# Down's first half with the seven-product scheme applied twice, weights held in the array and results turned in squares of 32

## The chip, the cores and the metric

The kernel runs on one core of one Trainium2 chip. The metric is device time in microseconds of one execution, as a median over runs. Of the core's engines, TensorE (PE in the profile) multiplies, loading one 128x128 operand into its array (PEld, "held" or "stationary" below) and streaming the other through it; VectorE (DVE), ScalarE (ACT) and GpSimd (POOL) do elementwise work; SyncE (SP) issues the DMAs here, in the order of its queue. Everything is float32.

## The reference

Eight blocks of 512 tokens by 512 features. Cut to what matters:

```python
xn = layernorm(x)
# linear attention
q, k, v = (einsum("bld,ed->ble", xn, W) + b for W, b in ((Wq, bq), (Wk, bk), (Wv, bv)))
kv = cumsum((elu(k) + 1) * v, axis=1)
s = einsum("bld,ed->ble", (elu(q) + 1) * kv * 32 ** -0.5, Wo) + bo
# gated feed-forward, 512 -> 2 x 2048 -> 512, each input rotated by signs and a Hadamard transform
h = fwht(xn * SU_ug) / 64
h = silu(h @ W_gate.T * (scale_gate * 64)) * (h @ W_up.T * (scale_up * 64))
g = fwht(h * SU_dp) / 64 @ W_down.T * (Wscale_dp * 64)
out = x + s * silu(g)
```

The kernel folds signs, transforms and the Down scales into the weights as it starts, so that each projection is one matrix product. "Down" is the product with `W_down`: 2048 hidden features in, 512 out.

## The kernel before

The eight blocks are worked in four pairs, p = 0 to 3; pairs follow each other without a break. In a pair come the attention's projections, four hidden units u = 0 to 3 (each is a gate and an up projection for a quarter of the hidden features, SiLU and product), the output projection after u = 0, the first half of Down after u = 1 (`down(p, 0, ...)`, over the hidden features of units 0 and 1), and the second half after u = 3, which adds the first half's result, applies the gate and writes the output.

All large products go by the seven-product scheme: a product of 2x2 blocks with 7 instead of 8 block products, named P1 to P7 (`P1, P2, P7, P3, P4, P5, P6 = range(7)`, L18). Each operand is kept as its seven "factors" (blocks, sums and differences of blocks), and running sums of products give the four result blocks.

The scheme is used at one or two levels:

- *Hidden units of pairs 1 to 3* (`by_blocks`, L947, and `block_product`, L678, matmul at L686) use two levels: seven outer products, each of seven inner ones. Weights are held and tokens stream. An outer product's inner sums sit in three PSUM tiles `px`, `py`, `pz`; `px` collects P1, P6, P5, P3 one on top of another and is read out in between by `read` (ScalarE copy, or VectorE addition where an earlier outer product is to be added), and `output` adds such a reading and `py` or `pz` into the result (L691 to L727). Results lie features by tokens.
- *Down* (`down`, L1001, through `token_groups`, L568, matmul at L584) uses one level: 7 products x 4 blocks of the contraction x 2 token groups x 2, each matmul 128x128 by 128x256. Here the tokens are held and the weights stream, so that results lie tokens by features, as input and output do. In the first half the sums are read by ScalarE copies (L593) and added by VectorE in 128x512 pieces (L599). The two finished results `dn`, 1 MB each, go to DRAM by one DMA each (`put_by`, L881), and are fetched for the second half (`fetch`, L886).

What a hidden unit leaves, `ho` (L983 to L991), is a tile of two feature blocks x seven token factors x 512 tokens. After each outer product `gated` (L985) is called for a finished result: SiLU on ScalarE, product and subtractions on GpSimd, or on VectorE for the last ones of a unit that stands ahead of Down. `by_blocks` itself has two sums on GpSimd, `u3 = u1 + v` (L961) and `v += r` (L965).

*Order of work.* The instructions of an engine run in program order, and a list `agenda` (L475 to L492) decides the order: `at(place, fn)` puts a step some number of places ahead, `advance(n)` runs the steps up to a place; one place is about a block product. `pace`, `later` and `nearest` slip waiting VectorE work in behind given instructions. `block_product` puts its seven products at places 0, 2, 3, 4, 8, 12 and 13 and advances by 7 only, so that products of neighbouring outer products mix and VectorE has time to empty a sum.

*Weights* come from DRAM, in the order of `queue` (L1219): `get_w` (L1259) asks for three ahead, `stream_w` (L341) issues the load on SP into the pool `wpool` of four buffers. A factor of the hidden units' weights (`w_gu`) is 896 KB, one of Down's (`w_down`) 512 KB.

*Pools.* `t8` has six 1 MB tiles, for the results and the sums; `xin` has one tile `x`, through which each block of tokens passes to be normalized (`normalized`, L190: load, layernorm on VectorE, store to `d_x`). Those tokens come back turned by 32x32 squares: `next_tokens` (L245) loads `z` in pieces of 128 bytes (32 values), and VectorE transposes each 32x32 square, which together turn the block. The loads of `z` are 256 KB each.

In pair 1, while Down's first half runs, `factors_kv` (L440) makes the second-level factors of the key and value weights: loads of `d_k` and `d_v`, seven stores to `d_kv` per part of which four wait for VectorE's sums.

## Time and profile before

| what | us |
|---|---|
| median of 3 runs (1535.12, 1537.55, 1537.87) | 1537.55 |
| the profiled execution | 1536.37 |
| its span | 1534.5 |
| granted TensorE clock, mean | 0.997 |
| Down's first half in pair 1, 2, 3: stretch of the trace | 627.96 to 678.89, 986.50 to 1037.40, 1345.00 to 1396.00 |
| median landing of a `w_gu` load (896 KB) / a `w_down` load (512 KB) | 4.5 / 4.6 |
| median landing of a `z` load (256 KB in 128-byte pieces) | 6.1 |
| median landing of a `d_d` store (1 MB) / its fetch | 7.4 / 5.7 |

The page gives each engine's busy time over the span and in 40 equal slices, the chain of work that ended last, and groups of instructions by line with their busy time, the mean duration of one, the idle time before them and what ended it. A float32 matmul appears as two records. The profiled execution is 1.2 us under the median.

### The profile page before, as it was taken

The numbers are of one execution on the slowest core, as the hardware profiler recorded it, in microseconds if no ns is written. First come the engines' busy times: TensorE is split into PE (matmuls) and PEld (weight loads), VectorE is DVE, ScalarE is ACT, GpSimd is POOL, SyncE is SP. The second block draws the span as 40 slices with busy tenths as digits, with TensorE's granted clock in tenths as the row PEclk, the third lists the DMA queues.
The fourth block names the chain that finished last, engine by engine and source line by source line (L and its number), as shares of the span: only waits on it lengthen the run. The fifth ranks groups of instructions, "written<-read, shape, count | busy, mean of one in ns | idle before, by whom it ended". The sixth has DMA issues, their size and how long they took to land.

```text
span 1534.5 us, 16212 instructions
## 1 busy us (share of the span) xinstructions
PE 1513.9 (99%) x6092; PEld 1154.2 (75%) x6092; DVE 1046.2 (68%) x1571; ACT 414.7 (27%) x668; POOL 360.5 (23%) x188
## 2 busy tenths in 40 slices
PE   7999999999999999999999999999999999999998
PEld 3446546747874688888885888888886888888887
DVE  8999788469777665636767895715675697633673
ACT  4462341232125411112115232111212332111211
POOL 1000000000320261205511235302621128200631
PEclk9999999999999999999999999999999999999999
DMA  8345778798975244784586644335484443525462
GB/s 275 96 149 170 237 273 238 228 300 280 271 282 141 96 145 176 239 275 164 167 269 217 188 144 162 116 119 182 172 247 154 142 144 113 185 93 183 160 259 81
DMA packets 213726, 288.93 MB, mean 188 GB/s; under 512 B 57488, under 2 KB 169360, under 8 KB 209424
## 3 DMA queue, kind: packets, MB, share of 16 engines
q1 hardware_dynamic: 213504, 287.87, 58.7%
q8 instruction: 48, 0.79, 0.2%
q14 instruction: 30, 0.25, 0.1%
q10 hardware_dynamic: 144, 0.03, 0.0%
HBM read 205.42 MB, written 82.44 MB: 188 GB/s over the span
## 4 chain that ended last, share of the span: by engine, by line
PE 82%; DVE 11%; DMA 4%; issue 1%; ACT 1%; POOL 0%; SPq 0%; POOLq 0%; DVEq 0%; ACTq 0%
PE px_gu L686 17%; PE px_dn L584 12%; PE pz_gu L686 9%; PE pz_dn L584 6%; PE py_gu L686 4%; PE py_dn L584 4%; PE px_kv L686 3%; PE px_o L584 3%; PE px_q L508 3%; PE px_gate L508 2%; PE pz_o L584 2%; PE pz_kv L686 2%; PE pz_q L508 2%; PE px_k L508 1%; PE px_v L508 1%
## 5 line engine op out<-in xcount | busy, mean ns | idle before, releaser
L686 PE MATMUL px_gu<-xo,w_gu 128*128 128x256 f32 x1456 | 348.4, 380 | 0.7 <-DVE sa_gu L696 0.6
L686 PEld LDWEIGHTS px_gu<-xo,w_gu 128*128 128x128 f32 x1456 | 275.2, 190 | 44.3 <-issue 2.4
L961 POOL TENSOR_TENSOR u_gu<-u_gu,v_gu 128x1024 f32<-128x1024 f32 x26 | 61.2, 2376 | 753.0 <-DVE u_gu L727 697.5
L584 PE MATMUL px_dn<-w_down,ho 128*128 128x256 f32 x1024 | 228.8, 379 | 0.9 <-DVE ho L93 0.9
L584 PEld LDWEIGHTS px_dn<-w_down,ho 128*128 128x128 f32 x1024 | 194.5, 190 | 29.4 <-issue 1.9
L686 PE MATMUL pz_gu<-xo,w_gu 128*128 128x256 f32 x728 | 187.4, 380 | 0.5 <-DVE u L524 0.4
L686 PEld LDWEIGHTS pz_gu<-xo,w_gu 128*128 128x128 f32 x728 | 137.6, 190 | 21.2 <-DVE a_gu L700 0.9
L584 PE MATMUL pz_dn<-w_down,ho 128*128 128x256 f32 x496 | 112.5, 379 | 0.6 <-DVE u L524 0.6
L584 PEld LDWEIGHTS pz_dn<-w_down,ho 128*128 128x128 f32 x496 | 93.8, 190 | 15.4 <-issue 1.2
L686 PE MATMUL py_gu<-xo,w_gu 128*128 128x256 f32 x364 | 93.7, 379 | 0.0
L1018 POOL TENSOR_TENSOR s<-s,d 128x512 f32<-128x512 f32 x30 | 40.0, 1332 | 166.0 <-ACT d L1017 166.0
L686 PEld LDWEIGHTS py_gu<-xo,w_gu 128*128 128x128 f32 x364 | 69.2, 190 | 9.4
L965 POOL TENSOR_TENSOR v_gu<-v_gu,r_gu 128x1024 f32<-128x1024 f32 x26 | 60.8, 2361 | 22.8 <-DVE r_gu L727 22.8
L508 PE MATMUL px_q<-xo,w_q 128*128 128x512 f32 x128 | 59.8, 593 | 0.3 <-ACT sa_q L520 0.3
L584 PE MATMUL px_o<-w_o,co 128*128 128x256 f32 x256 | 59.2, 380 | 0.3 <-DVE sa_o L595 0.3
L1017 ACT ACTIVATE d<-d 128x512 f32<-128x512 f32 x31 | 19.5, 630 | 144.9 <-DVE d L599 124.7
L584 PE MATMUL py_dn<-w_down,ho 128*128 128x256 f32 x256 | 57.9, 379 | 0.0
L989 ACT ACTIVATE a_gu<-a_gu,cols_sb 128x512 f32<-128x512 f32 x26 | 18.6, 720 | 142.2 <-DVE a_gu L727 140.8
L983 POOL TENSOR_TENSOR ho<-ho 128x1024 f32<-128x1024 f32 x24 | 56.3, 2357 | 1.4
L584 PEld LDWEIGHTS px_o<-w_o,co 128*128 128x128 f32 x256 | 48.3, 190 | 8.9 <-issue 1.0
L989 ACT ACTIVATE u_gu<-u_gu,cols_sb 128x512 f32<-128x512 f32 x52 | 36.6, 719 | 67.8 <-DVE u_gu L727 64.9
L584 PEld LDWEIGHTS py_dn<-w_down,ho 128*128 128x128 f32 x256 | 48.6, 190 | 6.6
(322 smaller groups left out, 2403.5 us busy)
## 6 DMA issues: line engine op xcount, KB each, us to landing
w_gu<-d_gu SPq DMA_DIRECT2D x91, 896.0 KB, 4.5
w_down<-d_down SPq DMA_DIRECT2D x56, 512.0 KB, 4.6
w_kv<-d_kv SPq DMA_DIRECT2D x14, 896.0 KB, 4.6
d_s<-o SPq DMA_DIRECT2D x8, 1024.0 KB, 6.3
d_d<-dn SPq DMA_DIRECT2D x8, 1024.0 KB, 7.4
d<-d_d SPq DMA_DIRECT2D x8, 1024.0 KB, 5.7
s<-d_s SPq DMA_DIRECT2D x8, 1024.0 KB, 8.7
y<-in_x_dram SPq DMA_DIRECT2D x8, 1024.0 KB, 7.6
```

The costliest lines, as they stand in the source:

```text
L508: nc.tensor.matmul(p.rearrange("p a t -> p (a t)") if len(r.shape) == 2 else p, ws[k][:, i, :], r, start=(first and k == 0), stop=(k == n ...
L584: nc.tensor.matmul(p[:, c], t[:, (2 * g + c) * P : (2 * g + c + 1) * P], ws[i](k), start=(first and k == 0 and c == cs[0]), stop=(k == n - ...
L686: nc.tensor.matmul(p[:, lane], w[:, lane, i, :], x[:, i, :], start=(first and lane == 0), stop=True, skip_group_check=True,)
L961: nc.gpsimd.tensor_tensor(r[:, m], ru1[:, m], rv[:, m], ALU.add)
L965: nc.gpsimd.tensor_tensor(rv[:, m], rv[:, m], rr[:, m], ALU.add)
L983: eng.tensor_tensor(ho[:, :, c], ho[:, :, a], ho[:, :, b], ALU.subtract)
L989: nc.scalar.activation(g[:, m], g[:, m], AF.Silu, scale=col("w_gate", u + m * NU + a * NG))
L1017: nc.scalar.activation(d, d, AF.Silu)
L1018: (nc.vector if final and (a, s) == (1, 0) else nc.gpsimd).tensor_tensor(r, r, d, ALU.mult)
```

## The change

For p = 1, 2, 3 Down's first half no longer calls `down(p, 0, ...)` but `down_by_blocks(p, ...)`. It applies the scheme twice, through the same `block_product`: seven outer products (in the order `IN_TURN`) of seven inner ones of two matmuls each (`two_terms`). The weights are now held and the tokens stream; a sum is 128x256 (one "lane"). Pair 0 and the second halves stay as they are.

- The second-level factors of the weights, `dl`, seven of 896 KB, are made once, in pair 1's attention (`factors_down`, at places 7, 20, 33, ...): for each, four loads of 128 KB out of `d_down`, four VectorE operations on 128x256, and one store. They pass through the tile `x` of `xin`.
- The second-level factors of the tokens are made in place in `ho`, and in halves of two `t8` tiles: per outer product n three subtractions of 128x512 and one more (`last_factor`), on GpSimd, except the first three for n = 1, which are on VectorE. Those of n = 0 stand ahead of the end of hidden unit 1.
- Sums over outer products: `read` and `output` on 128x256, and two additions of 128x1024 on VectorE (`with_u1`, `with_r`).
- Results now lie features by tokens. `turned` lets VectorE transpose each 32x32 square (two operations of 128x512 for each of four results) into a part of `ho` that is free, and eight DMAs for each result, of 64 KB in pieces of 128 bytes, put the squares at their places in `d_d`, which is now laid out tokens by features; `fetch` reads it accordingly.

```diff
@@ -16,6 +16,7 @@
 P1, P2, P7, P3, P4, P5, P6 = range(7)
+IN_TURN = (P1, P5, P6, P2, P7, P3, P4)
 @with_exitstack
@@ -345,6 +346,9 @@
             nc.sync.dma_start(w, inner[u][:, i])
         elif name[0] == "kv":
             nc.sync.dma_start(w, inner["kv"][:, name[1]])
+        elif name[0] == "dl":
+            assert name[1] in down_made
+            nc.sync.dma_start(w, inner["dl"][:, name[1]])
         elif name[0] == "down":
             h, i = name[1]
             assert wd_made[h] == 4
@@ -470,6 +474,34 @@
         at(8, plain)
         at(14, make)
+    down_made = set()
+    def factors_down(i):
+        if "dl" not in inner:
+            inner["dl"] = dram.tile([P, 7, 2, 7, P], F32, tag="d_dl", name="d_dl")
+        t = xin.tile([P, 3, 7, P], F32, tag="x", name=f"f_dl_{i}")
+        w = t.rearrange("p c s e -> p (c s e)")[:, : 2 * 7 * P].rearrange("p (m s e) -> p m s e", m=2, s=7)
+        for c in range(2):
+            for u in range(2):
+                nc.sync.dma_start(
+                    w[:, :, (P1, P2, P7, P4)[2 * c + u]], wd[0][:, i, 2 * u : 2 * u + 2, c * P : (c + 1) * P]
+                )
+        def encode():
+            for o, a, b, op in (
+                (P5, P7, P4, ALU.add), (P6, P5, P1, ALU.subtract), (P3, P2, P6, ALU.subtract), (P7, P1, P7, ALU.subtract)
+            ):
+                later(0.42, nc.vector.tensor_tensor, w[:, :, o], w[:, :, a], w[:, :, b], op)
+            later(0.0, store)
+        def store():
+            nc.sync.dma_start(inner["dl"][:, i], w)
+            down_made.add(i)
+        at(6, encode)
     agenda = []
@@ -675,21 +707,32 @@
         between()
-    def block_product(name, w, x, out, add, done, time=0):
-
-
-        px, py, pz = (bank(t, name, 2) for t in ("px", "py", "pz"))
-        sums = {}
-
+    def two_lanes(w, x):
         def product(p, i, first):
             for lane in range(2):
                 nc.tensor.matmul(
                     p[:, lane], w[:, lane, i, :], x[:, i, :],
                     start=(first and lane == 0), stop=True, skip_group_check=True,
                 )
+        return product
+    def two_terms(w, x):
+        def product(p, i, first):
+            for k in range(2):
+                nc.tensor.matmul(
+                    p[:, 0], w[:, k, i, :], x(k, i),
+                    start=(first and k == 0), stop=(k == 1), skip_group_check=True,
+                )
+        return product
+    def block_product(name, product, lanes, out, add, done, time=0):
+        px, py, pz = (bank(t, name, 2)[:, :lanes] for t in ("px", "py", "pz"))
+        sums = {}
         def read(what, m, q):
-            s = snap.tile([P, 2, H], F32, tag="s", name=f"{what}_{name}")
+            s = snap.tile([P, 2, H], F32, tag="s", name=f"{what}_{name}")[:, :lanes]
             if add is None:
                 nc.scalar.copy(s, px)
             else:
@@ -885,7 +928,8 @@
     def fetch(name):
         t = t8.tile([P, NT, D], F32, tag="t", name=name)
-        nc.sync.dma_start(t.rearrange("p n d -> p (n d)"), kept[name])
+        d = kept[name]
+        nc.sync.dma_start(t, d.rearrange("(n p) d -> p n d" if d.shape[0] == L else "p (n d) -> p n d", n=NT))
         return t
@@ -950,7 +994,7 @@
             return t8.tile([P, 2, 2, 2, H], F32, tag="t", name=f"{what}_{p}_{name}")
         def outer(i, out, add=None, done=None):
-            block_product(f"{name}_{p}_{i}", weights(i), xo[:, i], out, add, done, time)
+            block_product(f"{name}_{p}_{i}", two_lanes(weights(i), xo[:, i]), 2, out, add, done, time)
         ra = new("a")
         rest = {}
@@ -1045,6 +1089,107 @@
         if half == 0:
             for s in range(2):
                 put_by(f"d_{p}_{s}", ds[s])
+    def down_by_blocks(p, hos, get_w):
+        ds = [dram.tile([L, D], F32, tag=f"d_d_{p}_{s}", name=f"d_d_{p}_{s}") for s in range(2)]
+        h0, h1 = hos
+        room = []
+        def halves(what):
+            t = t8.tile([P, 2, 4 * H], F32, tag="t", name=f"{what}_{p}_dl")
+            return [t[:, i] for i in range(2)]
+        def result(t):
+            return t.rearrange("p (m l q t) -> p m l q t", m=2, l=1, q=2)
+        def block(a, q, o):
+            return (h0, h1)[a][:, :, o, q * H : (q + 1) * H]
+        places = {}
+        def factors(n):
+            o = IN_TURN[n]
+            eng = nc.vector if n == 1 else nc.gpsimd
+            if n < 3:
+                r = room[n].rearrange("p (i m t) -> p i m t", i=2, m=2)
+                x, y = r[:, 0], r[:, 1]
+            else:
+                x, y = (block(0, q, IN_TURN[n - 3]) for q in range(2))
+            b = block
+            eng.tensor_tensor(x, b(1, 1, o), b(0, 1, o), ALU.subtract)
+            eng.tensor_tensor(b(0, 1, o), b(0, 1, o), b(0, 0, o), ALU.subtract)
+            eng.tensor_tensor(y, b(1, 1, o), b(0, 1, o), ALU.subtract)
+            places[n] = {
+                P1: b(0, 0, o), P2: b(1, 0, o), P7: x, P6: y, P5: b(0, 1, o), P3: b(1, 1, o), P4: b(1, 0, o)
+            }
+        def last_factor(n):
+            b = block(1, 0, IN_TURN[n])
+            nc.gpsimd.tensor_tensor(b, b, places[n][P6], ALU.subtract)
+        stored = []
+        def turned(t, a, s):
+            o = (P5, P1)[len(stored) // 2]
+            z = h1[:, len(stored) % 2, o : o + 2]
+            stored.append((a, s))
+            def store():
+                d = ds[s].rearrange("(i t) (c j f) -> j t c i f", t=32, j=4, f=32)
+                for m in range(2):
+                    for j in range(4):
+                        nc.sync.dma_start(
+                            d[j][:, 2 * a + m],
+                            z[32 * j : 32 * j + 32, m].rearrange("p (i f) -> p i f", f=32),
+                        )
+            for m in range(2):
+                at(1 + 2 * m, lambda m=m: nc.vector.transpose(z[:, m], t[:, m, 0].rearrange("p q t -> p (q t)")))
+            at(4, store)
+        def outer(n, out, add=None, done=None):
+            i = IN_TURN[n]
+            w = get_w("dl", i)
+            block_product(
+                f"dl_{p}_{i}", two_terms(w, lambda k, j: places[n][j][:, k]), 1, out, add, done, 1.5
+            )
+        u3, f0 = halves("u3")
+        room.append(f0)
+        factors(0)
+        at(0, lambda: room.extend(halves("xy")))
+        at(0, lambda: factors(1))
+        at(3, lambda: factors(2))
+        for n in range(3, 7):
+            at(7 * n - 7, lambda n=n: factors(n))
+        for n in range(7):
+            at(7 * n + 5, lambda n=n: last_factor(n))
+        ra, rv = halves("a")
+        ru1, rr = halves("u1")
+        ra, rv, ru1, rr, u3 = (result(t) for t in (ra, rv, ru1, rr, u3))
+        def plus(o, a, b):
+            o, a, b = (t.rearrange("p m l q t -> p (m l q t)") for t in (o, a, b))
+            nc.vector.tensor_tensor(o, a, b, ALU.add)
+        def with_u1():
+            plus(u3, ru1, rv)
+        def with_r():
+            plus(rv, rv, rr)
+            turned(rv, 1, 1)
+        outer(0, ra)
+        outer(1, rv)
+        outer(2, ru1, ra, with_u1)
+        outer(3, ra, ra, lambda: turned(ra, 0, 0))
+        outer(4, rr, ru1, with_r)
+        outer(5, u3, u3, lambda: turned(u3, 0, 1))
+        outer(6, ru1, rr, lambda: turned(ru1, 1, 0))
+        between()
+        for s in range(2):
+            kept[f"d_{p}_{s}"] = ds[s]
     def load_y(p, s):
         y = t8.tile([P, NT, D], F32, tag="t", name=f"y_{p}_{s}")
@@ -1232,7 +1377,10 @@
                 at_o = len(queue) - (2 if p == 0 else 0)
                 queue[at_o:at_o] = [(p, "o", 0), (p, "o", 1)]
             if u % 2:
-                queue += [(p, "down", (u // 2, i)) for i in (P1, P7, P2, P6, P5, P3, P4)]
+                if p and u == 1:
+                    queue += [(p, "dl", i) for i in IN_TURN]
+                else:
+                    queue += [(p, "down", (u // 2, i)) for i in (P1, P7, P2, P6, P5, P3, P4)]
     ahead = []
     def ask(n):
@@ -1347,6 +1495,9 @@
         if p:
             catch_up()
             inner_tokens(xo)
+            if p == 1:
+                for n, i in enumerate(IN_TURN):
+                    at(7 + 13 * n, lambda i=i: factors_down(i))
             co = hop.tile([P, 2, 7, L], F32, tag="h", name=f"co_{p}")
         heads_made = (attention if p < 2 else attention_by_blocks)(p, xo, co, get_w)
         more = p + 1 < B // 2
@@ -1387,7 +1538,10 @@
                     for i, (m, lo, hi) in enumerate((("k", 0, 4), ("k", 4, 7), ("v", 0, 4), ("v", 4, 7))):
                         at(2 + 12 * i, lambda m=m, lo=lo, hi=hi: factors_kv(m, lo, hi))
                 flush()
-                down(p, 0, hos, get_w)
+                if p:
+                    down_by_blocks(p, hos, get_w)
+                else:
+                    down(p, 0, hos, get_w)
                 hos = []
         flush()
         ds = [fetch(f"d_{p}_{s}") for s in range(2)]
```

## Prediction

> **What bounds the kernel now.** I read the page's first two parts, then the chain, the groups, and windows over the three stages that change.
>
> ```profile
> span 1534.5 us, 16212 instructions
> PE 1513.9 (99%) x6092; PEld 1154.2 (75%) x6092; DVE 1046.2 (68%) x1571; ACT 414.7 (27%) x668; POOL 360.5 (23%) x188
> PE   7999999999999999999999999999999999999998
> PE 82%; DVE 11%; DMA 4%; issue 1%; ACT 1%; POOL 0%; SPq 0%; POOLq 0%; DVEq 0%; ACTq 0%
> ...
> L584 PE MATMUL px_dn<-w_down,ho 128*128 128x256 f32 x1024 | 228.8, 379 | 0.9 <-DVE ho L93 0.9
> ```
>
> TensorE (PE) is busy throughout: nothing but matmul work can be saved, and what is saved stays saved only while the other engines keep up. The clock row reads 9 in every slice. The windows of Down's first half in pairs 1, 2 and 3 (columns: us; busy us and instructions of PE, PEld, DVE, ACT, POOL; clock; DMA share; GB/s) say the same:
>
> ```profile
> 627.96:678.89 50.93, 50.93 (x237) 44.78 (x236) 21.88 (x31) 7.46 (x12) 2.00 (x1) 1.00 0.76 236
> 986.50:1037.40 50.90, 50.90 (x238) 44.74 (x237) 13.88 (x17) 7.46 (x12) 2.07 (x1) 1.00 0.39 124
> 1345.00:1396.00 51.00, 51.00 (x238) 44.83 (x237) 13.86 (x17) 7.00 (x12) 1.49 (x1) 1.00 0.39 126
> ```
>
> The reader is to see that in the second and third, VectorE (DVE) is a quarter busy and GpSimd (POOL) idle; in pair 1 the encoding of the kv weights runs beside, with DVE at 43% and DMA at 0.76.
>
> **Removed: 14 matmuls a pair.** Before: 7 products x 4 contraction blocks x 2 token groups x 2 = 112 matmuls of 128x256. After: 7 outer x 7 inner x 2 terms = 98, same shape. A row's mean includes overlap, so I take the pitch, from the chain of waits inside the stage (start us, length):
>
> ```profile
> 654.88 17.27 PE px_dn L584 x80
> ```
>
> 80 records in 17.27 us are 0.2159 a record; an fp32 matmul leaves two records (the group L584 shows 1024 for 512 matmuls), so 0.4318 us. 14 x 0.4318 = 6.05 us a pair, 18.1 us in all. Weight loads become as many as the matmuls, as before. Nothing else in PE's work changes.
>
> **Start of each stage.** The first products need hidden unit 1 finished and folded a second time. The new factor operations stand on POOL between the adds L961 and L965 of unit 1, before "v += r", which delays the last SiLU, product and subtractions; outer 1's factors then follow on DVE. From the DVE rows before (L991 at 629.63 for 1.40 us, then L983) and POOL's 1.22 us, I placed these by hand in pair 1: PE finds an output not drained (0.3), a Y sum late (0.15) and two second-outer factors late (0.7). About 1.2 us a pair, 3.6 in all; zero to 2.5 a pair for the range.
>
> **POOL: 25 subtractions of 128x512 a pair, 3 more on DVE.** The nearest rows:
>
> ```profile
> 497.34 1.27 POOL L316 TENSOR_TENSOR co<-co 128x512 f32<-128x512 f32 x1 [2.96 <-DVE co L791]
> 498.57 1.26 POOL L318 TENSOR_TENSOR co<-co 128x512 f32<-128x512 f32 x1
> 499.79 1.27 POOL L317 TENSOR_TENSOR co<-co 128x512 f32<-128x512 f32 x1
> ...
> L1018 POOL TENSOR_TENSOR s<-s,d 128x512 f32<-128x512 f32 x30 | 40.0, 1332 | 166.0 <-ACT d L1017 166.0
> ```
>
> Back to back the pitch is 1.225; the L1018 mean, beside a busier DVE, is 1.33; single ones reach 1.64 and 2.19. 25 x 1.225 = 30.6 us lie in a stage of some 44 us. The tight place is the fifteenth: at 1.225 the third outer's last factor is ready some 1.5 us before PE wants it (about 650.5 against 652 in pair 1's times). At 1.33 it is 1.6 us later, even. I take nothing; at 1.6 us an operation the lateness is 15 x 0.375 - 1.5 = 4.1 us a pair. PE is what waits then, and the rest of the stage with it.
>
> **DVE.** Five outers read their sums with 7 additions of 128x256, two with 3 (the other reads are ScalarE copies, at 0.37 by L285): 41 x 0.42 = 17.2 us. Two additions of 128x1024 at 1.215 make 2.4, eight transposes at 0.683 make 5.5, the three factors 2.0 (0.68 each, the 128x512 addition): 27 us, where six additions of 0.69 stood (4.1).
>
> ```profile
> L307 DVE TENSOR_TENSOR xo<-xo 128x256 f32<-128x256 f32 x28 | 11.3, 419 | 9.0 <-PE pz_q L508 7.2 <-PE px_q L508 1.4 <-PE py_q L508 0.4
> L93 DVE STREAM_TRANSPOSE xo<-z 128x512 f32<-128x512 f32 x24 | 15.4, 683 | 0.0
> L983 DVE TENSOR_TENSOR ho<-ho 128x1024 f32<-128x1024 f32 x28 | 33.5, 1215 | 0.3
> ```
>
> In pairs 2 and 3, 13.9 + 23 = 37 us of some 45: hidden, since an inner product's two matmuls take 0.86 us and the list spaces an outer's products so that a drain has a product or more of time. In pair 1, 21.9 + 23 = 45 of 45: no room. Overlapped issue (pitch 0.60 where the 128x512 row says 0.69) gives back some 5 us.
>
> **Making the weights, once in pair 1's attention.** Per factor four loads of 128 KB, four DVE additions of 0.42 and a store of 896 KB; 28 x 0.42 = 11.8 us of DVE, beside PE in slices where DVE shows 6 or 7 tenths. They occupy the single `x` tile, which moves the loads and layernorms of blocks 4 and 5 (about 5.2 us of DVE each) into hidden unit 0 and the output projection, and the `z` loads of block 4 (128-byte pieces, 256 KB each) into the changed stage. The matmuls cover it; uncovered it would be 22 us. I put 1 us (0 to 4).
>
> **Weights and stores.** A pair's seven Down weights grow from 512 to 896 KB. Results leave by 32 stores of 64 KB in 128-byte pieces, four batches of eight, and on SP's queue after the batches stand, one each, the loads of unit 2's weights P5, P6, P2 and P7: SP takes its queue in order, so a batch whose transpose is late, or whose predecessors are still landing, holds up that load and then PE. No store before has pieces this small. Nearest rows:
>
> ```profile
> w_gu<-d_gu SPq DMA_DIRECT2D x91, 896.0 KB, 4.5
> ...
> z<-d_x SPq DMA_DIRECT2D x24, 256.0 KB, 6.1
> ...
> d_kv<-f_k SPq DMA_DIRECT2D x7, 256.0 KB, 4.2
> ```
>
> Four `z` loads in 128-byte pieces at 763 to 772 moved 145 to 147 GB/s with full DMA; so a 512 KB batch takes 512/145 = 3.6 us, within an outer's 98/7 x 0.4318 = 6.05. By hand the four weight loads land 2 to 4 us early. The other end: pieces at twice the price, 7.2 us a batch, over the period; the loads then come later by 4 us or so a pair, 8 in pair 1.
> The Trainium skill's page "DMA: Bandwidth & Descriptors", section Specifications, speaks against the change: it gives 512 bytes as the smallest transfer at line rate, with a read-modify-write below. The `z` row shows the lower rate for loads; no row here shows a store. If the rule means two passes for a store, the sum would be that of the stores' rival below.
>
> In pair 1 DMA is the fuller term. 236 GB/s x 50.93 us = 12.0 MB; seven times 384 KB of weights (2.75 MB) makes 14.8, of which 2.1 MB go at 145 GB/s (14.5 us) and the rest at 360 GB/s, which that stretch reaches in its best slices (35 us): 50 us against 45. DVE waits there for `d_kv` stores to land (7.9 us idle in 640 to 648, harmless so far), and behind those waits now stand the drains PE needs. Some stores may slip past the stage, so 0 to 5 us; I take 2.5.
>
> **Sum.** -18.1 + 3.6 + 1 + 2.5 = -11.0. The profiled execution's 1536.37 becomes 1525.4; the median shown, 1537.55, lies 1.2 above it, so 1526.5.
>
> **Rivals.**
> - *All of it comes through.* For: PE at 100% in the windows, POOL idle there, DVE a quarter busy. Against: the late factors at the start. 1537.55 - 18.1 = 1519.5.
> - *POOL sets the pace.* With DVE at 80% or more beside it, an operation takes 1.6 us; 3 x 4.1 = 12.4 us of waits: 1539. For: the single rows of 1.64 and 2.19, beside DVE work. Against: the mean of 1.33, which alone gives 0.4 us or so more. At 1.45 us it is 1526.5 + 3 x 1.9 = 1532.
> - *The 128-byte stores hold up unit 2's weights* (the slower side). Place: PE's first product of gu_2 on each of P5 to P7. Price: pieces at twice the loads' cost, 4.4 + 4.4 + 8 = 17 us: 1543.5. It decides from where a batch takes over 6 us, and turns the sign where it costs over 11 us. For: no such store is in the trace, `z` runs at a third of the weight loads' rate. Against: the weights are asked 4 us ahead.
> - *It does not do what it says:* the matmuls replaced are counted above, so only a second use of the new weights in the wrong place could leave the saving out; excluded by the code.
>
> **Chances.** 0.2% (3.1 us) is about what a measurement of this kernel tells from no change. The forecast's case 0.44 (its own range 1522.5 to 1532); all saved 0.14; POOL 0.17, of which a bit over half ends within 3 us of before and the rest faster; stores, with DMA in pair 1 worse than 5 us, 0.25, nearly all slower. Faster: 0.44 + 0.14 + 0.07 = 0.65; same 0.11; slower 0.24. The range: below, half of the all-saved case; above, up to 1542, which leaves out some 0.12 of the stores' case.
>
> **What would show it.** Matmuls fewer by 42 (84 records); the three stages some 44 to 47 us instead of 51; PE's waits for DVE of about 1 us at each stage's start and none on POOL; drains of 128x256 at 0.42; POOL at 1.23 to 1.33; the store batches under 6 us from issue to landing; in pair 1 waits of up to 5 us, in 2 and 3 below 2. PE waiting for a `w_gu` DMA just behind the stage means the stores' rival; for POOL in the third and fourth outer, POOL's; waits in pair 1's attention or hidden unit 0 would put the making of the weights above its 1 us.

## The result and the profile after

The changed kernel takes 1560.11 us (median of 4 runs, 1559.11 to 1563.46) against 1536.89 for the kernel before (4 runs): a ratio of 1.0156, 95% interval 1.0138 to 1.0175. It is slower by 23 us where 11 us less was forecast, and above the top of the forecast's range, 1542. The page of the changed kernel:

```profile
span 1557.8 us, 16546 instructions
PE 1507.0 (97%) x6008; PEld 1139.2 (73%) x6008; DVE 1143.8 (73%) x1743; ACT 408.0 (26%) x668; POOL 472.0 (30%) x263
...
PE 71%; DVE 14%; DMA 4%; POOL 3%; SPq 3%; issue 2%; ACT 2%; POOLq 0%; DVEq 0%; ACTq 0%
```

PE has 84 records fewer, the 42 matmuls that the change removes. They are worth 18.1 us, yet the span is 23.3 longer: 41 us were lost. In the chain, POOL and SP's queue now stand with 3% each where they had nothing. What PE waited for (us in total, times, longest):

```profile
PE px_gu L713 <- DMA w_gu<-d_gu: 6.8, 3, 2.7
PE pz_o L616 <- DVE u_gu L743: 5.3, 1, 5.3
PE px_gu L713 <- DVE sc_gu L739: 3.7, 4, 1.1
PE pz_dl L722 <- DVE a_dl L743: 3.0, 3, 1.0
PE py_dl L722 <- DVE a_dl L743: 2.0, 2, 1.0
PE pz_gu L713 <- DVE u_gu L743: 1.8, 3, 0.6
PE px_dl L722 <- ACT sc_dl L737: 1.4, 3, 0.5
PE px_dl L722 <- DVE xy_dl L1122: 1.1, 3, 0.4
PE pz_dl L722 <- POOL ho L1129: 1.1, 1, 1.1
```

Three groups are to be seen: a single wait of 5.3 at the output projection (`pz_o`), three waits for weights of a hidden unit, and small waits for VectorE that come three times, once a pair. The timeline puts a place to each. I compare three stretches of both traces: pair 1 from its first key product to its first Down matmul; and, for each of pairs 1 to 3, from the first matmul of Down's first half to the first of its second half, which takes in hidden units 2 and 3 ("the long stretch" below).

| stretch, us | before | after | difference |
|---|---|---|---|
| pair 1, keys to Down | 448.77 to 627.96: 179.19 | 447.65 to 634.72: 187.07 | +7.9 |
| long stretch, pair 1 | 627.96 to 760.99: 133.03 | 634.72 to 783.06: 148.34 | +15.3 |
| long stretch, pair 2 | 986.57 to 1119.60: 133.03 | 1008.16 to 1142.06: 133.90 | +0.9 |
| long stretch, pair 3 | 1344.48 to 1477.51: 133.03 | 1366.91 to 1500.81: 133.90 | +0.9 |

With 6.05 us of matmuls gone from each long stretch, pairs 2 and 3 lost 6.9 each and pair 1 lost 21.4 there, besides the 7.9 in its attention and hidden units 0 and 1. (The rest of the two spans differs by -1.7 us in all, -1.1 of it before pair 1.) So three losses need an explanation: one that every pair has, one that only pair 1's Down has, and the making of the weights.

**The loss of every pair** lies at the stage's start. Windows over pair 3 (us; busy us and instructions of PE, PEld, DVE, ACT, POOL; clock; DMA share; GB/s):

```profile
1344.48:1366.91 22.43, 22.43 (x105) 19.75 (x104) 17.54 (x27) 2.16 (x3) 14.80 (x8) 1.00 0.48 160
1366.91:1390.30 23.39, 18.41 (x77) 13.78 (x76) 20.29 (x22) 5.77 (x12) 18.13 (x11) 1.00 0.36 118
1390.30:1416.20 25.90, 25.90 (x121) 22.80 (x120) 16.82 (x36) 0.37 (x1) 17.26 (x14) 1.00 0.64 172
```

All of it is in the middle row: PE idle for 5.0 of 23.4 us, and 77 records where 23.39 / 0.2159 = 108 fit, 6.7 us of work. VectorE and GpSimd are both busy there. What they do, first VectorE, then GpSimd, from the timeline (start, duration, line):

```profile
1369.62 2.25 DVE L1035 TENSOR_TENSOR ho<-u_gu 128x1024 f32<-128x1024 f32 x1 [1.81 <-ACT u_gu L1033]
...
1372.40 1.21 DVE L1027 TENSOR_TENSOR ho<-ho 128x1024 f32<-128x1024 f32 x1
1373.53 0.67 DVE L743 TENSOR_TENSOR u_gu<-sc_gu,pz_gu 128x512 f32<-128x512 f32 x1
1374.13 3.10 DVE L1027 TENSOR_TENSOR ho<-ho 128x1024 f32<-128x1024 f32 x2
1377.16 1.75 DVE L1120 TENSOR_TENSOR xy_dl<-ho,ho 128x512 f32<-128x512 f32 x1
1378.83 0.41 DVE L743 TENSOR_TENSOR a_dl<-sa_dl,py_dl 128x256 f32<-128x256 f32 x1
1379.16 1.42 DVE L1121 TENSOR_TENSOR ho<-ho 128x512 f32<-128x512 f32 x1
```

```profile
1368.43 2.36 POOL L1035 TENSOR_TENSOR ho<-v_gu 128x1024 f32<-128x1024 f32 x1 [0.83 <-ACT v_gu L1033]
1373.75 1.27 POOL L1129 TENSOR_TENSOR ho<-ho,u_dl 128x512 f32<-128x512 f32 x1 [2.96 <-PE px_gu L713]
1376.18 2.18 POOL L1120 TENSOR_TENSOR xy_dl<-ho,ho 128x512 f32<-128x512 f32 x1 [1.16 <-DVE ho L1027]
1378.43 1.59 POOL L1121 TENSOR_TENSOR ho<-ho 128x512 f32<-128x512 f32 x1
```

Lay the two on one another. VectorE's L1035 begins at 1369.62, while GpSimd's L1035 runs until 1370.79; from there to its end at 1371.87 is 1.08, about its duration alone (1.21). GpSimd's L1120 begins at 1376.18 while VectorE's second L1027 runs until 1377.23, and ends 1.13 later; VectorE's L1120 begins at 1377.16, and ends 0.55 after GpSimd's has ended at 1378.36. Each waits for the other's running instruction. The L743 rows in between take 0.67 and 0.41 as always: they read one operand from PSUM. So these instructions, which take both operands from SBUF, *take turns* on the two engines, one whole instruction at a time. In the kernel before, GpSimd had 2 us of work in these stages, and the two met once, for 0.35 us (its L991 is the changed kernel's L1035, its L983 the L1027):

```profile
1344.12 2.38 POOL L991 TENSOR_TENSOR ho<-v_gu 128x1024 f32<-128x1024 f32 x1 [0.83 <-ACT v_gu L989]
...
1346.15 1.42 DVE L991 TENSOR_TENSOR ho<-u_gu 128x1024 f32<-128x1024 f32 x1 [0.79 <-ACT u_gu L989]
...
1349.83 2.35 DVE L983 TENSOR_TENSOR ho<-ho 128x1024 f32<-128x1024 f32 x2
```

The rest of the changed kernel's trace says the same. Of VectorE's tensor_tensor instructions with both operands in SBUF, those that began with more than 0.25 us of a GpSimd operation still to run took 1.41 to 2.26 us for 128x1024 (19 of them) and 1.10 to 1.75 for 128x512 (14); all others took at most 1.23 and 0.69. With one operand in PSUM, 298 of 128x512 and 59 of 128x256 began so, and none took more than 0.69 and 0.43.

**The making of the weights.** The `x` tile is taken, and the layernorm of block 4 comes while the output projection runs, beside three 128x1024 subtractions of GpSimd. VectorE, then GpSimd:

```profile
565.11 0.75 DVE L155 TENSOR_SCALAR x<-x,mv,rstd 128x512 f32<-128x512 f32 x1
565.78 0.68 DVE L627 TENSOR_TENSOR sa_o<-px_o,bo_r 128x512 f32<-128x512 f32 x1
566.38 6.93 DVE L155 TENSOR_SCALAR x<-x,mv,rstd 128x512 f32<-128x512 f32 x3
573.23 0.68 DVE L770 TENSOR_TENSOR u_gu<-px_gu,r_gu 128x512 f32<-128x512 f32 x1
```

```profile
565.65 7.38 POOL L1027 TENSOR_TENSOR ho<-ho 128x1024 f32<-128x1024 f32 x3
```

L155 has a median of 0.54; here three take 6.93, one for each of GpSimd's instructions (7.38 / 3 = 2.46). The drains behind them (L770, then L743) come 5 us late, and PE stands at `pz_o` for 5.3. The clock then is not full (windows of the same trace):

```profile
560.00:580.00 20.00, 14.68 (x58) 12.27 (x57) 14.91 (x17) 7.45 (x9) 16.60 (x8) 0.83 0.43 145
690.00:710.00 20.00, 14.91 (x58) 12.07 (x57) 8.72 (x16) 3.41 (x6) 0.00 (x0) 0.88 0.99 231
```

At 0.2159 us a record 92.6 fit into 20 us. The 58 of the first window are 34.6 too few, 7.5 us of work, for 5.3 us of idle time: the granted clock, 0.83 on average, takes the rest.

**The loss of pair 1's Down.** The second of these windows shows it: PE waits for `w_gu`. SP's queue there (start, time of the issues):

```profile
679.10 0.81 SPq L346 DMA_DIRECT2D w_gu<-d_gu  x1
679.96 1.47 SPq L452 DMA_DIRECT2D f_v<-d_v  x2
681.52 8.15 SPq L1142 DMA_DIRECT2D d_d<-ho  x8
689.78 1.02 SPq L458 DMA_DIRECT2D d_kv<-f_v  x2
690.89 0.50 SPq L346 DMA_DIRECT2D w_gu<-d_gu  x1
691.48 1.30 SPq L458 DMA_DIRECT2D d_kv<-f_v  x2
692.83 7.20 SPq L1142 DMA_DIRECT2D d_d<-ho  x8
700.07 1.62 SPq L458 DMA_DIRECT2D d_kv<-f_v  x3
701.79 0.47 SPq L346 DMA_DIRECT2D w_gu<-d_gu  x1
```

The loads of `w_gu` leave 11.8 and 10.9 us apart, where an outer product, of a hidden unit as of Down, has 7 x 2 matmuls and lasts 6.05: the weights come at about half the pace at which PE can use them. A batch of eight stores holds the queue for 7 to 8 us and kv stores for 1 to 3 more. Whether it is the pieces, the bytes or the number of DMAs is for the runs.

### The profile page after: what moved, and what is told of

Its sections match the earlier page's. It is cut to its first block, busy times and chain, and to the rows that moved or that the text cites. A ratio compares the mean times of both kernels' runs of the same rounds, so it can differ in the third digit from the quotient of the medians.

```text
span 1557.8 us, 16546 instructions
## 1 busy us (share of the span) xinstructions
PE 1507.0 (97%) x6008; PEld 1139.2 (73%) x6008; DVE 1143.8 (73%) x1743; ACT 408.0 (26%) x668; POOL 472.0 (30%) x263
## 4 chain that ended last, share of the span: by engine, by line
PE 71%; DVE 14%; DMA 4%; POOL 3%; SPq 3%; issue 2%; ACT 2%; POOLq 0%; DVEq 0%; ACTq 0%
PE px_gu L713 13%; PE px_dn L616 7%; PE pz_gu L713 6%; PE py_gu L713 3%; PE pz_dn L616 3%; PE px_q L540 3%; PE px_kv L713 3%; PE px_o L616 3%; PE px_gate L540 2%; PE px_dl L722 2%; PE py_dn L616 2%; PE px_up L540 2%; PE pz_o L616 2%; PE pz_kv L713 2%; PE px_k L540 1%
## 5 line engine op out<-in xcount | busy, mean ns | idle before, releaser
L1005 POOL TENSOR_TENSOR u_gu<-u_gu,v_gu 128x1024 f32<-128x1024 f32 x26 | 61.2, 2373 | 630.7 <-DVE u_gu L770 569.7
L713 PEld LDWEIGHTS pz_gu<-xo,w_gu 128*128 128x128 f32 x728 | 139.2, 192 | 23.3 <-DVE u_gu L743 3.8
L616 PE MATMUL px_dn<-w_down,ho 128*128 128x256 f32 x640 | 143.0, 379 | 1.8 <-DVE ho L94 1.8
L616 PEld LDWEIGHTS px_dn<-w_down,ho 128*128 128x128 f32 x640 | 121.5, 190 | 20.3 <-DVE ho L94 2.2
L722 PE MATMUL px_dl<-ho,w_dl 128*128 128x256 f32 x300 | 75.1, 386 | 3.0 <-ACT sc_dl L737 1.4
L616 PE MATMUL pz_dn<-w_down,ho 128*128 128x256 f32 x304 | 69.1, 379 | 0.6 <-DVE u L556 0.6
L722 PEld LDWEIGHTS px_dl<-ho,w_dl 128*128 128x128 f32 x300 | 57.2, 193 | 14.0 <-ACT sc_dl L737 2.6
L1009 POOL TENSOR_TENSOR v_gu<-v_gu,r_gu 128x1024 f32<-128x1024 f32 x26 | 60.9, 2363 | 18.2 <-DVE r_gu L770 18.2
L616 PEld LDWEIGHTS pz_dn<-w_down,ho 128*128 128x128 f32 x304 | 57.5, 190 | 10.3 <-issue 1.2
L1027 POOL TENSOR_TENSOR ho<-ho 128x1024 f32<-128x1024 f32 x24 | 56.6, 2367 | 1.4
L737 ACT COPY sa_gu<-px_gu 128x512 f32<-128x512 f32 x26 | 15.1, 581 | 157.9 <-PE px_gu L713 129.1
```

The lines of the kernel that those rows point to most:

```text
L616: nc.tensor.matmul(p[:, c], t[:, (2 * g + c) * P : (2 * g + c + 1) * P], ws[i](k), start=(first and k == 0 and c == cs[0]), stop=(k == n - ...
L713: nc.tensor.matmul(p[:, lane], w[:, lane, i, :], x[:, i, :], start=(first and lane == 0), stop=True, skip_group_check=True,)
L722: nc.tensor.matmul(p[:, 0], w[:, k, i, :], x(k, i), start=(first and k == 0), stop=(k == 1), skip_group_check=True,)
L737: nc.scalar.copy(s, px)
L1005: nc.gpsimd.tensor_tensor(r[:, m], ru1[:, m], rv[:, m], ALU.add)
L1009: nc.gpsimd.tensor_tensor(rv[:, m], rv[:, m], rr[:, m], ALU.add)
```

## The experiments

Each line gives the median, the ratio to the kernel before on the same chip with its interval, and the long stretches of pairs 1, 2, 3 (before: 133.0 each; changed kernel: 148.3, 133.9, 133.9). "Keys to Down" is pair 1's first stretch (before 179.2, changed kernel 187.1).

**e1, only the making.**

```diff
-                if p and u == 1:
+                if False and u == 1:
...
-                if p:
+                if False:
                     down_by_blocks(p, hos, get_w)
```

> The weights' second-level factors are made in pair 1 as in the changed kernel, but every pair keeps the one-level Down. Theory 1 (layernorm of block 4, moved beside GpSimd's products in the output projection, costs its 5.3 us wait and the slow clock after it): about 1545 us, 8 over before, with the same wait of PE at pz_o. Rival (the making is hidden, all of the loss is in the new stage): 1537 to 1539. My recorded forecast for this part was 1 us.

1545.87, 1.0056 (1.0036 to 1.0076); stretches 133.1, 133.0, 133.0; keys to Down 186.9. The making alone costs 7.7 us there, with the wait of 5.3 at `pz_o` and three L155 in 6.93 as before. The rival falls.

**e2, the making in another tile.**

```diff
-        t = xin.tile([P, 3, 7, P], F32, tag="x", name=f"f_dl_{i}")
...
+        t = t8.tile([P, NT, D], F32, tag="t", name=f"f_dl_{i}")
...
```

> The changed kernel with the weights' factors made in a tile of the result pool instead of the single tile x, so that blocks 4 and 5 are normalized where they were before. Theory 1: the 5.3 us wait at pz_o goes, and the loads of z leave pair 1's new stage; 1552 if only the first matters, 1545 if the z loads also were what delayed the w_gu weights. Rival (the place of the layernorm does not matter): 1560.

1555.78, 1.0126 (1.0105 to 1.0146); keys to Down 181.5, so 5.5 of the 7.9 are gone with the wait at `pz_o`. Pair 1's long stretch is 147.0: the displaced loads of `z` had no more than 1.3 us of it.

**e3, the stores in pieces of 2 KB.**

```diff
-                d = ds[s].rearrange("(i t) (c j f) -> j t c i f", t=32, j=4, f=32)
+                d = ds[s].rearrange("(n p) d -> p n d", p=P)
...
-                            d[j][:, 2 * a + m],
-                            z[32 * j : 32 * j + 32, m].rearrange("p (i f) -> p i f", f=32),
+                            d[32 * j : 32 * j + 32, 2 * a + m], z[32 * j : 32 * j + 32, m]
```

> The 32 stores of each pair write the same bytes from the same tiles in pieces of 2 KB, so the squares are not put in place and the result differs. Theory 2 (the 128-byte stores delay unit 2's weights in pair 1): the three waits for w_gu (6.8 us) and the low clock after them go, 11 us less, 1549; pairs 2 and 3 do not change. Rival (DMA in pair 1 is full of kv factors, z and larger weights whatever the pieces): 1556 to 1560.

1558.91, 1.0141 (1.0122 to 1.0159); 146.5, 133.9, 133.9. The size of the pieces is worth 1.9 us in pair 1 and nothing in the others. My forecast's rival had the place right and the cause wrong. The rule of the Trainium skill that I weighed against the change (page "DMA: Bandwidth & Descriptors", section Specifications: no line rate below 512 bytes) hardly shows in the time here.

**e4, the new stage in pairs 2 and 3 only** (`if p > 1` in the two places of e1).

> Pair 1 keeps the one-level Down; pairs 2 and 3 use the new one; the weights are made in pair 1 as in the changed kernel. Theory: before + 8 (the making) + 2 x 0.9 (each later pair loses 6.9 us to waits against 6.05 saved): 1547. Rival (each new stage costs a third of the 23 us, 7.7 us): 1552.

1546.55, 1.0066 (1.0042 to 1.0091); 133.2, 133.9, 133.9; keys to Down 185.7. The losses add up from separate places.

**e5, the kv factors later.**

```diff
-                        at(2 + 12 * i, lambda m=m, lo=lo, hi=hi: factors_kv(m, lo, hi))
+                        at(52 + 12 * i, lambda m=m, lo=lo, hi=hi: factors_kv(m, lo, hi))
```

> The changed kernel with the kv weights' factors of pair 1 begun 50 places later, behind the new stage, in hidden units 2 and 3. Theory 2b (what pair 1's new stage loses beyond the others is that DMA and VectorE are full there with kv factors, not the 128-byte pieces): pair 1's stage with the two units behind it falls from 148.3 to about 134 us, as in pairs 2 and 3, the waits for w_gu go, and the whole is 1546. Rival (the larger weights and stores alone are too much for DMA right behind attention): stays over 1555.

1565.81, 1.0193 (1.0178 to 1.0209); 154.5, 133.9, 133.9. The waits for `w_gu` are gone, and pair 1 runs from its first Down matmul to unit 2's first in 49.3 us, as pairs 2 and 3 do (52.6 in the changed kernel). So the kv factors beside the new stage are what sets pair 1 apart. But in units 2 and 3 they cost more than they did: PE waits some 14 us there for drains that come late on VectorE. Most stand behind L465, which waits for its stores to land, and of which the last two take 4.13 beside GpSimd's L1027 (0.57 each alone); the longest wait, 5.3, lies behind a sum of GpSimd's (L1005) that is late itself. Moved, not solved.

**e6 and e7, GpSimd's subtractions left out.**

```diff
+            if n in (1,):
                 eng.tensor_tensor(x, b(1, 1, o), b(0, 1, o), ALU.subtract)
                 eng.tensor_tensor(b(0, 1, o), b(0, 1, o), b(0, 0, o), ALU.subtract)
                 eng.tensor_tensor(y, b(1, 1, o), b(0, 1, o), ALU.subtract)
+            else:
+                x, y = b(1, 1, o), b(0, 1, o)
```

(The indentation of the three lines is not shown as a change. e7 has `(0, 1)`; the last factors go with theirs, in e6 all seven.)

> GpSimd's 25 second-level token subtractions of each pair are left out (raw blocks are used in their place); VectorE's three remain. Theory 3 (GpSimd and VectorE slow each other when both read and write SBUF, and the first GpSimd operations also delay the end of unit 1): in pairs 2 and 3 VectorE's L1027 is back at 1.21 and L1120 to L1122 at 0.7, the seven waits at the stage's start go, stage with the units behind it from 133.9 to 127.5 us; whole some 1545 or less. Rival (PE waits because the two-matmul products are too short for VectorE's drains): 132 or more.

1539.79, 1.0025 (1.0016 to 1.0035); 141.5, 128.05, 128.05. VectorE in pair 3 of e6:

```profile
1354.44 1.42 DVE L1035 TENSOR_TENSOR ho<-u_gu 128x1024 f32<-128x1024 f32 x1 [0.79 <-ACT u_gu L1033]
...
1358.11 2.35 DVE L1027 TENSOR_TENSOR ho<-ho 128x1024 f32<-128x1024 f32 x2
1360.39 0.68 DVE L1121 TENSOR_TENSOR xy_dl<-ho,ho 128x512 f32<-128x512 f32 x1
1360.99 0.41 DVE L743 TENSOR_TENSOR a_dl<-sa_dl,py_dl 128x256 f32<-128x256 f32 x1
```

The same instructions: 2.25 is 1.42, 3.10 is 2.35, 1.75 is 0.68. The stage is 5.0 us shorter than before the change, of 6.05 that the matmuls are worth: without GpSimd beside it the stage does what was forecast, and short products and drains are no bound. (1.42 is still 0.2 over the 1.21 of an instruction alone, as in the kernel before.)

> As e6, but the first outer product's subtractions (n = 0, on GpSimd ahead of unit 1's last sums) and its last factor are kept, those of n = 2 to 6 left out. Theory 3 splits: the first two waits of a stage (1.1 for sc_gu, 0.6 for u_gu) stay, as GpSimd's product of unit 1 still falls beside VectorE's, the later ones (1.0, 0.4, 0.4, 1.0) go: about 130 us in pairs 2 and 3 where the changed kernel has 133.9. Rival (the delay comes from the first three alone, and the rest follows from it): 133.

1547.57, 1.0073 (1.0058 to 1.0088); 142.7, 130.4, 130.4. Of the 5.85 us that GpSimd's work costs a pair, 2.3 come with the first outer product's operations and 3.5 with the later ones. Leaving work out takes away its turns and its own time on GpSimd together, and no run separates the two. The rows show both: in pair 3 the first three subtractions put unit 1's last product on GpSimd 1.9 us later against the stage's start (from 0.4 ahead of it to 1.5 behind), while PE waits for GpSimd itself only once in all, for 1.1 us, otherwise for VectorE, and 0.5 a pair for ScalarE.

**e8, the first three on VectorE** (`eng = nc.vector if n < 2 else nc.gpsimd`).

> The changed kernel with the first outer product's three subtractions on VectorE in place of GpSimd, so that GpSimd's sums and product of unit 1 are not delayed. Theory 3: VectorE's L1035 at the stage's start back from 2.25 to 1.4, the first two waits go, pairs 2 and 3 at 131 to 132 us instead of 133.9, whole about 1556. Rival (VectorE is the one short of time there; two more us on it cost as much as they bring): 133.5 to 135.

1558.83, 1.0148 (1.0133 to 1.0163); 145.9, 132.0, 132.0. The stretch is 1.9 shorter, but the one ahead of it 2.2 longer (pair 3, output projection to Down: 72.9 against 70.8). The stretch is what the theory expected, 131 to 132, but the whole is not: one of the moved subtractions takes 2.53 beside GpSimd's L1009, and PE waits 1.4 for the drain behind it. For the whole the rival holds: on VectorE the work costs as much as it brings.

**e9, one store a result.**

```diff
-                d = ds[s].rearrange("(i t) (c j f) -> j t c i f", t=32, j=4, f=32)
-                for m in range(2):
-                    for j in range(4):
-                        nc.sync.dma_start(
-                            d[j][:, 2 * a + m],
-                            z[32 * j : 32 * j + 32, m].rearrange("p (i f) -> p i f", f=32),
-                        )
+                d = ds[s].rearrange("(n p) d -> p n d", p=P)
+                nc.sync.dma_start(d[:, 2 * a : 2 * a + 2], z)
```

> Each result of the new stage is stored by one DMA of the same 512 KB instead of eight, so the squares are not put in place and the result differs. Theory 2c (the loads of w_gu stand on SP's queue behind eight stores that take 6.5 to 8 us to issue in pair 1, and behind kv stores): with seven issues fewer a batch the waits for w_gu and the low clock go, pair 1's stage with the units behind it from 148.3 to 137 or less, whole about 1549. Rival (bytes: DMA is full in pair 1 whatever the number of DMAs): 145 or more, 1557, as with eight stores in 2 KB pieces.

1552.79, 1.0109 (1.0096 to 1.0122); 140.7, 133.9, 133.9. The same bytes in one DMA instead of eight, which also has pieces of 2 KB, bring 7.6 us in pair 1, against 1.9 for larger pieces alone (e3): 5.7 are left for the number of DMAs. SP's queue in e9:

```profile
680.09 1.13 SPq L346 DMA_DIRECT2D w_gu<-d_gu  x1
681.26 1.41 SPq L452 DMA_DIRECT2D f_v<-d_v  x2
682.78 1.10 SPq L1140 DMA_DIRECT2D d_d<-ho  x1
684.23 2.26 SPq L458 DMA_DIRECT2D d_kv<-f_v  x2
686.58 2.01 SPq L346 DMA_DIRECT2D w_gu<-d_gu  x1
```

The second `w_gu` leaves 6.5 us after the first, not 11.8, the third still 10.0 after the second (10.9), the fourth 5.2 after the third (8.3). PE's waits for `w_gu` fall from 6.8 to 3.0. 133.9 is not reached, nor is 137; e14 has more on the rest.

**e10, the stores on ScalarE's queue** (`nc.scalar.dma_start`).

> The changed kernel with the 32 stores issued on ScalarE's queue instead of SP's, same pieces. Theory 2c: the loads of w_gu go out on time, waits for them gone or under 2 us in pair 1; ScalarE is a quarter busy, so little is lost there: 1549 to 1552. Rival (bandwidth, or the 128-byte pieces): waits for w_gu as in the changed kernel, 1558 or more.

1578.31, 1.0273 (1.0260 to 1.0286); 155.1, 140.6, 136.8. Worse throughout: PE waits 13 us for ScalarE's copies `sa_gu` and `sb_gu` (L737), which now stand behind the issues. That waits for `w_gu` stay at 5.2 us speaks for some share of the bytes.

**e11, one subtraction early.** `b01 - b00` uses unit 0 alone and is moved to GpSimd's idle time ahead of the stage (in pair 3 at 1314.6 to 1328.2, the stage begins at 1361.3); then `y = b11 - b01`, `x = y - b00`.

```diff
+                        at(2 + 2 * n, lambda b=hos[0][:, :, i]: nc.gpsimd.tensor_tensor(b[:, :, H:], b[:, :, H:], b[:, :, :H], ALU.subtract))
...
-            eng.tensor_tensor(x, b(1, 1, o), b(0, 1, o), ALU.subtract)
-            eng.tensor_tensor(b(0, 1, o), b(0, 1, o), b(0, 0, o), ALU.subtract)
             eng.tensor_tensor(y, b(1, 1, o), b(0, 1, o), ALU.subtract)
+            eng.tensor_tensor(x, y, b(0, 0, o), ALU.subtract)
```

> The changed kernel with one of the three subtractions of each outer product (the one of unit 0 alone) done on GpSimd early in hidden unit 1, and x taken as y minus the first block: 7 of 28 operations a pair leave the stage's start. Theory 3 (instructions of GpSimd and VectorE with two SBUF operands take turns): pairs 2 and 3 at 131 to 132.5 instead of 133.9, all 1556. Rival (the first sums' drains set the start, not the turns): 133.5 or more.

1550.55, 1.0096 (1.0082 to 1.0111); 144.3, 131.7, 130.2. A quarter of the subtractions out of the start gives back 2.2 and 3.7 us, and the stage of pairs 2 and 3 is now 1.3 to 2.8 us shorter than before the change. Why the two pairs differ is not shown.

**e12, e13, e15, e16, e17: towards a better version.** All have pair 1 as before the change and e11's order in pairs 2 and 3, where every one of them has 130.2 to 131.7 us. They differ in where the weights' factors are made, in the program and in the trace. e12 asks for them here, in the tile `x`; e13 asks at u = 2 and moves the layernorms; e15 is e13 with the additions on GpSimd. e12's place:

```diff
+                if p == 1 and u == 3:
+                    for n, i in enumerate(IN_TURN):
+                        at(2 + 7 * n, lambda i=i: factors_down(i))
```

> A version after what the runs showed: pair 1 keeps the one-level Down, the weights' factors are made in pair 1's last hidden unit, when x is free, and pairs 2 and 3 have the early subtraction of e11. By the theories: making costs 0 to 2 us in place of 7.8, pairs 2 and 3 gain 0.5 to 2 us each: 1533 to 1537. Rival (the additions of 128x256 wait for GpSimd there too): 1540 or more.

1544.02, 1.0049 (1.0035 to 1.0063). The place asked for is not the place in the trace: six of the seven factors are made at 485 to 557, in pair 1's attention and hidden unit 0, as in the changed kernel (466 to 538) but behind the layernorms of blocks 4 and 5, and only the seventh at 785, beside the second half of Down. So the agenda does not fix the order of such work, and the last hidden unit was not tried. Keys to Down 181.2, and pair 2's first query products wait 5.5 us: the loads of `z` stand behind the last factor in the tile `x` and end at 803, and the encoding of the tokens (L94) runs from 812 to 820.

> As e12 (pair 1 one-level, pairs 2 and 3 by blocks with the early subtraction), but the weights' factors are made behind the layernorms of blocks 4 and 5 and ahead of the loads of z for pair 2. Theory: making costs nothing then, pairs 2 and 3 gain 2.8 us each as in e11: 1537 - 5.6 = 1531 to 1532. Rival (the additions on VectorE cost their share wherever they stand): 1535 or more.

1538.77, 1.0020 (1.0008 to 1.0031): keys to Down 187.8. All seven are made at 485 to 574 here, again not in unit 2. Additions of 0.42 fell beside GpSimd's products of unit 0:

```profile
565.97 2.58 DVE L105 TENSOR_TENSOR f_dl<-f_dl 128x256 f32<-128x256 f32 x1 [1.97 <-DMA f_dl<-d_down]
568.48 0.68 DVE L627 TENSOR_TENSOR sa_o<-px_o,bo_r 128x512 f32<-128x512 f32 x1
569.08 1.97 DVE L105 TENSOR_TENSOR f_dl<-f_dl 128x256 f32<-128x256 f32 x1
```

Another shape, the same lengthening.

> As e13, with the 28 additions of the weights' factors on GpSimd in place of VectorE. Theory (turns between the two engines are the whole cost of the making): pair 1 as before the change, pairs 2 and 3 2.8 us shorter each as in e13, 1531 to 1533. Rival (tile x, the loads and stores or the delay of GpSimd's own queue cost it): 1536 or more.

1539.51, 1.0032 (1.0020 to 1.0043): keys to Down 188.1, the making at 483 to 559, no such additions on VectorE any more, but a wait of 4.8 for a `w_gu` load and 0.8 for `w_o` behind the factors' loads and stores on SP's queue.

> Pair 1 one-level, pairs 2 and 3 by blocks with the early subtraction (as e12 to e15), the weights' factors made in pair 1's hidden units 2 and 3 in tiles of the result pool, additions on VectorE. If the making only costs by what it displaces: 1 us or less in units 2 and 3, whole 1531 to 1533, below the kernel before. Rival (the additions meet GpSimd's long products there too, about 1.5 us each for up to 28): 1537 or more.

(The making from place 4 of unit 2 on, every 12 places, in tiles of `t8`; in the trace at 691 to 753, in units 2 and 3.) 1542.04, 1.0043 (1.0026 to 1.0060): keys to Down 179.2, as before the change, but pair 1's long stretch 143.6; additions of up to 2.6 us beside GpSimd's products there.

> As e16, with the 28 additions of the weights' factors on GpSimd, most of them in the first three outer products of units 2 and 3 of pair 1, where it is idle. If turns between the engines were what the making cost in e16, units 2 and 3 are back near 133 us with Down before them, and the whole is 1531 to 1534. Rival (loads and stores on SP's queue hold up w_gu loads there as in e15): 1536 or more.

(Four factors from place 1 of unit 2, three from place 1 of unit 3, additions on GpSimd; in the trace at 668 to 746.) 1543.10, 1.0054 (1.0040 to 1.0068): 143.7 in pair 1, now with 7.0 us of waits for `w_gu` loads. No version beat the kernel before. Turns between the engines are in the rows of e13 and e16; e12, e15 and e17 have other waits. Counted as the median's distance from the kernel before, plus what pairs 2 and 3 gain, the making costs 8 to 13 us in each. Why both places, the attention and units 2 and 3, cost about as much is not settled.

**e14, one store and no subtractions on GpSimd** (e6 and e9 together).

> The changed kernel with one store a result (as e9) and without GpSimd's token subtractions (as e6); the result differs. If stores on SP's queue and turns between GpSimd and VectorE are all that pair 1 loses beyond pairs 2 and 3, its stage with the units behind it is 128 to 130 us; if the kv factors' traffic has a share of its own, 133 or more. Pairs 2 and 3: 128 as in e6.

1533.57, 0.9980 (0.9970 to 0.9989); 131.7, 128.0, 128.0. Between the two expectations: together the two parts give back 16.6 of the 20.3 us that lie between 148.3 and 128.0; 3.7 stay, 2.6 of them as waits for `w_gu`. So the kv factors' own traffic has a share, a small one. With e5 this says that in pair 1 it is the meeting of the two on SP's queue that costs most: without the kv factors there the waits for `w_gu` go (e5), and with one store a result they fall by more than half (e9). This run leaves out a part of the computation and is no version.

## Why the prediction was wrong

- *Removed: 14 matmuls a pair, 6.05 us.* Right: 84 records fewer, and with GpSimd's subtractions left out 5.0 of the 6.05 us appear in pairs 2 and 3 (e6, e14).
- *"POOL ... I take nothing" and "DVE ... 27 us ... hidden".* This step failed. I priced each engine's instructions by their durations alone, added them up by engine, and found each below the stage's length. But the two lists run one after the other where both read two operands from SBUF. I quoted GpSimd's rows of 1.64 and 2.19 "beside DVE work" and took them for slow GpSimd instructions in a rival; that VectorE waits as well, and by a whole instruction, was not in any case. GpSimd's 25 subtractions, which I took at nothing, cost 5.85 us a pair (133.9 to 128.05, e6), and 6.8 in pair 1: nearly the whole of the saving. How much of it is turns alone and how much GpSimd's own time no run says.
- *Start of each stage, 1.2 us a pair.* The place was right, the size was 5.0 us idle and 6.9 lost, mostly for the same reason: I had moved the instructions with their old durations. Without GpSimd's subtractions 1.1 of the 6.05 stay lost (e6), near my 1.2; that it is the same 1.2 is not shown.
- *Making the weights, 1 us (0 to 4).* Measured 7.7 (e1). I counted 11.8 us of additions as covered and saw that layernorm and loads move, but did not ask what they would meet: three L155 beside three products of GpSimd. The wait of 5.3 also lowered the clock.
- *Weights and stores.* I priced a batch by its bytes, 3.6 us, against 6.05. The price in pair 1 is that of eight issues in the queue, 6.5 to 8.2 us, and kv stores between them. In pairs 2 and 3 the batches take 4.6 to 7.0 us, and PE never waited for `w_gu`.
- *In pair 1 ... 0 to 5 us; I take 2.5.* Measured 14.4 beyond the other pairs. Of that, 7.6 go with one store in place of eight (e9), 1.9 of them by the larger pieces alone (e3).
- *The rivals.* None was it. The rival with the stores had the right sign and one of the right waits, but it asked for all pairs and for the pieces' price (and its "third of the weight loads' rate" does not come out of the rows shown: 256 KB in 6.1 us is a fifth of 896 KB in 4.5, and 145 GB/s is two fifths of 360); "POOL sets the pace" had a share of the right cause with the wrong bearer.

## What to carry to other kernels

Before work is moved to an idle engine, look at where its operands lie: in this case GpSimd's work was free beside VectorE's additions out of PSUM, but with two SBUF operands on both sides the durations add. A row of the trace gives a price only for the company it was measured in, and the few long ones in a group with a tight median are the first thing to explain. A store that is cut into many DMAs is priced by its issues on the queue, and by what stands behind them, as well as by its bytes.

## What the hardware showed that was not expected

- VectorE's and GpSimd's operations with both operands in SBUF take turns by whole instructions: VectorE's 128x1024 in 1.21 alone and 2.25 beside GpSimd; a 128x256 addition of 0.42 in up to 2.58; GpSimd's 128x512 in 1.27 and up to 2.25. Additions with one operand in PSUM kept 0.41 and 0.67 in the same microseconds. The Trainium skill's page "GPSIMD Engine Reference", section Specifications, says that GpSimd's SBUF interfaces are shared with VectorE, with contention for VectorE's instructions in a two-port mode or with two SBUF inputs; the trace agrees for two SBUF inputs. L155, with one tensor operand, also waited: 0.54 alone, 6.93 for three. Other instructions with one SBUF operand did not: five 128x512 transposes that began beside GpSimd's subtractions took 0.69 to 0.71, as elsewhere.
- A single wait of 5.3 us cost more than itself: the granted clock in the 20 us around it was 0.83, and 7.5 us of matmuls were missing for 5.3 us of idle time. Two waits of 2.7 and 2.4 us (690 to 710) left it at 0.88; in pair 3's window 1366.91 to 1390.30, 5.0 us of idle time in waits of at most 1.1 left it at 1.00.
- Eight stores of 64 KB in 128-byte pieces took 6.5 to 8.2 us to issue on SP's queue in pair 1, and in pieces of 2 KB still 5.3 to 6.6 (e3); one DMA of the same 512 KB took 0.7 to 1.4 (e9). Most of the time on the queue goes by the number of DMAs.
